# Four gated layers on one core: the first stage's loads and normalising move to ScalarE, and the last attention clears ahead, keeps GpSimd in written order and splits keys from queries

## The chip, the core and the metric

The kernel runs on one core of a Trainium2 chip. The core has five engines, each of which runs its own stream of instructions in order: TensorE (PE in the profile, with its weight loads as PEld), VectorE (DVE), ScalarE (ACT), GpSimd (POOL) and SyncE (SP, which here only issues DMAs). They wait for each other through semaphores. Plain loads and stores are issued by SP and ScalarE; gathers by index are issued by GpSimd. The metric is the device time of one execution, in microseconds.

## The reference, cut to what matters

Sixteen sequences of 128 tokens with 256 features (`x`) pass four layers. Each layer adds a cross part and then a feed-forward part to `x`, each scaled by the tanh of a gate:

```python
x = x + tanh(g_xattn[0]) * L0_xattn(ctx, ctx, layernorm(x), ssm_kernel, D, 8)   # first stage
x = x + tanh(g_ffn[0])   * L0_ffn(layernorm(x), ...)                            # experts
x = x + tanh(g_xattn[1]) * L1_xattn(layernorm(x), ctx, ctx, mask, ...)
x = x + tanh(g_ffn[1])   * L1_ffn(layernorm(x), ...)
x = x + tanh(g_xattn[2]) * L2_xattn(layernorm(x), ctx, ctx, decay)
x = x + tanh(g_ffn[2])   * L2_ffn(layernorm(x), ...)                            # experts
x = x + tanh(g_xattn[3]) * L3_xattn(layernorm(x), ctx, ...)                     # channel attention
x = x + tanh(g_ffn[3])   * L3_ffn(layernorm(x), ...)
```

Two of them matter here. The first stage forms, for each head of 8 features, all 64 products of context features, runs a causal convolution over the 128 tokens with the head's kernel (plus `D` times the input), and contracts the result with the normalised `x` as query. The channel attention takes the transposed view: each of the 16 heads has 8 of the 128 token rows as channels, and attends from 256 feature positions to 256 feature positions:

```python
q, k, v = Wq @ x + bq, Wk @ c + bk, Wv @ c + bv      # per sequence, [128, 256]; x normalised
scores = einsum('bhkt,bhks->bhts', q, k) / sqrt(8)   # 16 heads, 8 channels, 256 x 256
out = Wo @ (softmax(scores) applied to v) + bo
```

The queries come from `x`, the keys and values from the context alone.

## The kernel before, in words

**The frame.** The program holds `x` in SBUF as four groups `xg[g]` of four sequences each. The body, `passage`, is written twice: a first time with softmax sums watched for range, and a second time, under a condition on the result, with a search for the maxima (`search`). On these inputs only the first runs; "search" branches are not executed. Outside blocks marked `manual_schedule`, a planner orders each engine's instructions by its own estimate of their costs. Inside such a block, the engines named there keep the order in which the code is written, and the planner orders the others. Tiles come from pools with a number of buffers; an instruction that writes a buffer waits until the last reader of its former content is done.

**First stage (`stage_l0x`, L200 to L312; the planner orders it).** SP issues the four loads of `x` (L93), constants (L99), and four loads of the padded kernels (L213) into `rev`, which shares memory with `oT`. ScalarE issues the two loads of the transposed context (L95), 1 MB each, and then applies Tanh to the gates (L113). TensorE reverses the kernels by a product with a flipped identity (L225, two heads each), ScalarE copies the result into `toep` (L226), VectorE adds `D` to its diagonal (L237). `layernorm` (L149) takes mean and variance of one group on VectorE (L155, L156), the reciprocal root on GpSimd (L160), and normalises on VectorE (L163) into `xn`; TensorE transposes `xn` (L234) and ScalarE copies it into `qT` (L235). Then the loop over 16 heads: GpSimd multiplies the context features (`kv`, L289), TensorE convolves (L297, twelve products of 512 columns a head) into `y` with three buffers in PSUM, VectorE multiplies by `qT` of all sequences (`pr`, L302) and reduces (L305). In between come the mask rows (L246 to L262) and key rows (L267, L269) for a later layer. At the end the result is transposed back and added to `x` (L310, L312).

**Channel attention (`stage_l3x`, L1478 to L1784; TensorE, VectorE and ScalarE keep the written order, the planner orders GpSimd and SP).** Its input still lacks the experts' output of the stage before, which lies in DRAM and is gathered here (`fetch`, L709, two gathers a sequence; three buffers of `yc`). For sequence `b`: `stats` adds the gathered rows (L1524) and takes statistics (L1527 to L1530); `rsqrt` is the reciprocal root on GpSimd (L1535); `normal` normalises (L1541); `project` makes queries and keys (L1553, L1554) into one PSUM tile; `biased` adds the biases (L1559, L1560); `halves` splits both into a rounded part (ScalarE, L1566) and its remainder (GpSimd, L1567) and writes them by four DMAs to the DRAM buffer `scr` (L1571, L1573); `spread` reads them back by four DMAs into `qas` and `kas` (L1589), in the layout that a head's product needs. These, and `vbuf` for the values, have three buffers; each must be zero outside the written rows, so `clear` (L1546 to L1549) zeroes each once and sets a column of ones in `vbuf`, from whose product the softmax sums come. `project_v` and `keep_v` make the values.

Each sequence has eight steps `u`. In each, `weigh` makes scores (L1660) into one of two PSUM buffers and ScalarE takes their exponential into `pt` (L1667). `values` multiplies by the values (L1676) once for every two steps; `keep_values` copies the result to `avs` (L1687); `back` transposes (L1692), `normalise` divides by the sums, `turn`, `output` and `store` bring the result to `x` (L1707 to L1725). Two tables say what else is issued at step `u` of sequence `b`: `taken` ahead of the step's scores, `made` behind them; `(halves, 3)` stands for `halves(b + 3)`:

```python
for n in range(-40, 8 * B + 17):
    b, u = divmod(n, 8)
    for f, d, *r in taken[u]: when(f, b + d, *r)
    if 0 <= n < 8 * B: weigh(n)
    for f, d, *r in made[u]: when(f, b + d, *r)
```

So the loop starts five sequences ahead, and TensorE's first scores stand behind the projections of the first three sequences.

Of the kernel before, what the change touches and what calls it, by code (L numbers as in the profile page):

```python
# [55 lines left out]
def passage(ctx: ExitStack, tc: tile.TileContext, a: dict, out: bass.AP, inv, flag):  # L56
# [56 lines left out]
    nc.scalar.activation(tg, tg, AF.Tanh)  # L113

# [34 lines left out]
    def layernorm(pool, g, extra=None, tag="xn"):  # L149
# [10 lines left out]
        nc.gpsimd.tensor_tensor(rs, ve, neghalf, ALU.pow)  # L160
        xn = pool.tile([P, GB, D], F32, name="xn", tag=tag)
        for k in range(GB):
            nc.vector.tensor_scalar(xn[:, k, :], x[:, k, :], mv[:, k, 0:1], rs[:, k : k + 1], ALU.subtract, ALU.mult)  # L163
# [36 lines left out]
    def stage_l0x(ka, vbuf, anyk):  # L200

        with tc.tile_pool(name="s0", bufs=1) as s0, tc.tile_pool(name="s0w", bufs=2) as s0w, tc.tile_pool(
# [9 lines left out]
            for q in range(4):  # L212
                nc.sync.dma_start(  # L213
                    rev[:, 4 * q : 4 * q + 4, :],
                    bass.AP(tensor=kp.tensor, offset=kp.offset + 4 * q * W, ap=[[1, P], [W, 4], [1, D]]),
                )
# [6 lines left out]
            for h in range(0, B, 2):  # L223
                t = pst.tile([P, 2 * D], F32, name="tp")
                nc.tensor.matmul(t, lhsT=flip, rhs=rev[:, h : h + 2, :].rearrange("p h s -> p (h s)"), start=True, stop=True)  # L225
                nc.scalar.copy(T[:, h : h + 2, :].rearrange("p h s -> p (h s)"), t)  # L226
            dsk = s0.tile([P, B], F32, name="dsk")
# [1250 lines left out]
    def stage_l3x(wn, bn, wv, won, bov, pos, wgt, ys):  # L1478
# [8 lines left out]
        with tc.tile_pool(name="l3", bufs=1) as l3, tc.tile_pool(name="l3w", bufs=2) as w_, tc.tile_pool(  # L1487
# [4 lines left out]
            engines={mybir.EngineType.PE, mybir.EngineType.DVE, mybir.EngineType.Activation}  # L1492
# [3 lines left out]
            scr = [l3d.tile([8, P, D], F32, name=f"scr{i}") for i in range(NB)]  # L1496
# [7 lines left out]
            def begin(b):  # L1504
                fetch(b)
# [37 lines left out]
            def clear(b):  # L1543

                if b < NB:
                    nc.vector.memset(qas[b].bitcast(F32), 0.0)  # L1546
                    for t in (kas[b].rearrange("p j t -> p (j t)"), vbuf[b].rearrange("p s h k -> p (s h k)")):
                        nc.scalar.activation(t, ones[:, 0:1].to_broadcast(list(t.shape)), AF.Copy, scale=0.0)
                    nc.gpsimd.memset(vbuf[b][:, :, :, 8:9], 1.0)  # L1549

            def project(b):
                ps["f", b] = t = psa.tile([P, 2, D], F32, name="qk", tag="a")
                nc.tensor.matmul(t[:, 0, :], lhsT=wn[0], rhs=xns.pop(b), start=True, stop=True)  # L1553
                nc.tensor.matmul(t[:, 1, :], lhsT=wn[1], rhs=cbs[b], start=True, stop=True)  # L1554

            def biased(b):
                t = ps.pop(("f", b))
                fs[b] = f = w_.tile([P, 2, D], F32, name="f")
                nc.vector.tensor_scalar(f[:, 0, :], t[:, 0, :], bn[0], SC, ALU.add, ALU.mult)  # L1559
                nc.vector.tensor_scalar(f[:, 1, :], t[:, 1, :], bn[1], None, ALU.add)  # L1560

            def halves(b):

                f = fs.pop(b)
                hl = w_.tile([P, 2, 2, D], F32R, name="hl")
                nc.scalar.copy(hl[:, :, 0, :], f)  # L1566
                nc.gpsimd.tensor_tensor(hl[:, :, 1, :], f, hl[:, :, 0, :].bitcast(F32), ALU.subtract)  # L1567
                s = scr[b % NB]
                hf = hl.bitcast(F32)
                for x in range(2):  # L1570
                    nc.sync.dma_start(s[2 * x : 2 * x + 2].rearrange("s p t -> p s t"), bc(hf[:, 0, x], 1, 2))  # L1571
                for x in range(2):
                    nc.sync.dma_start(s[4 + 2 * x : 6 + 2 * x].rearrange("s p t -> p s t"), hf[:, 1])  # L1573

            def spread(b):

                s = scr[b % NB]
                for h in range(2):
                    r = slice(64 * h + 32, 64 * h + 34)
                    if not search:  # L1580
                        continue
                    if b < NB:
                        nc.sync.dma_start(kas[b][r].bitcast(F32), bc(ones[0:2, :], 1, 16))
                    else:
                        nc.sync.dma_start(qas[b % NB][r].bitcast(F32), bc(zr, 1, 16))
                s = s.rearrange("s (k h) t -> (s k) (h t)", h=16)
# [478 lines left out]
```

## Time and profile before

| | us |
|---|---|
| median of 3 runs (lowest, highest) | 1079.42 (1078.66, 1079.55) |
| the profiled execution | 1077.04 |
| its span, first to last instruction | 1075.3 |
| first stage (0 to 138): PE, DVE, ACT, POOL busy | 111.6, 111.0, 17.0, 77.5 |
| channel attention (752 to 972): PE, DVE, ACT, POOL busy | 182.8, 107.2, 155.4, 72.2 |
| its entry (752 to 787): PE, DVE, ACT, POOL busy | 8.0, 14.1, 10.4, 16.4 |
| its steady part (800 to 905): PE, DVE, ACT, POOL busy | 99.6, 58.5, 81.2, 39.9 |
| mean granted TensorE clock | 0.904 |

A row of the timeline has the start in us, the duration in us, the engine, the line of the kernel, the operation, what it writes and reads, the shapes, a count of merged instructions, and in brackets how long the engine idled before it and what ended that. The windows give busy time per engine in a stretch. The chain is the work that ended last, followed back from the end. A matmul's end is modelled; GpSimd's times are rough.

### The profile page before, as it was taken

To read this page: it belongs to the slowest core of one execution; us is meant where nothing else is said; L and a number is where in the kernel's file an instruction comes from. 1 tells how busy PE (TensorE), PEld (TensorE's weight loads), DVE (VectorE), ACT (ScalarE), POOL (GpSimd) and SP (SyncE) were. 2 spreads that over 40 slices of the span, in tenths; PEclk is the share of its full clock that TensorE was granted. 3 is DMA by queue.
4 is the path that set the end of the run, shared out by engine and by line. 5 is a ranking of instruction groups with operands and counts; after the bars stand their busy time and mean duration, and the time that the engine had idled before them with its cause. 6 is when DMAs were issued, how large, how long until landed. Compare 5 with 4: busy or idle time off the path is not lost. (4 is left out here: it accounts for less than half of the span.)

```text
span 1075.3 us, 14892 instructions
## 1 busy us (share of the span) xinstructions
PE 904.1 (84%) x5212; PEld 602.5 (56%) x5212; DVE 607.5 (56%) x1537; ACT 456.8 (42%) x707; POOL 342.3 (32%) x389
## 2 busy tenths in 40 slices
PE   3899978899999888888864858998169999998797
PEld 1444456677778444455443747887145555555564
DVE  5988966322225656787788586454345555534442
ACT  1211024223322446666762242454257777882111
POOL 5766322543115324211111046550443342201000
PEclk9999979999999978999986557899579999997999
DMA  9100070233341109800000202352488887530000
GB/s 305 41 1 1 0 220 21 63 104 109 69 143 50 39 20 144 78 1 1 1 1 1 78 1 88 109 145 82 142 247 235 220 222 195 164 79 1 20 30 32
DMA packets 71401, 94.12 MB, mean 88 GB/s; under 512 B 9271, under 2 KB 63127, under 8 KB 69015
## 3 DMA queue, kind: packets, MB, share of 16 engines
q1 hardware_dynamic: 56952, 67.21, 21.1%
q0 software_dynamic: 14080, 23.78, 11.4%
q10 hardware_dynamic: 288, 2.10, 0.5%
q8 instruction: 45, 0.74, 0.3%
q14 instruction: 36, 0.29, 0.1%
HBM read 57.06 MB, written 33.55 MB: 84 GB/s over the span
## 5 line engine op out<-in xcount | busy, mean ns | idle before, releaser
L1667 ACT ACTIVATE pt<-s 128x1024 f32<-128x1024 f32 x128 | 126.4, 1024 | 32.5 <-PE s L1660 29.8
L709 POOL DMA_INDIRECT yc<-ys,pos x64 | 62.4, 975 | 125.0 <-DVE x L729 49.2
L297 PE MATMUL y<-kv,toep 128*128 128x512 f32 x192 | 86.6, 602 | 1.6 <-DVE toep L237 1.6
L1660 PE MATMUL s<-qa,ka 64*128 64x256 f32 x512 | 64.3, 332 | 8.3 <-ACT pt L1667 7.5
L1676 PE MATMUL av<-pt,v 128*32 128x256 f32 x1024 | 69.4, 389 | 0.1
L289 POOL TENSOR_TENSOR kv<-ctxT 128x1024 f32<-128x1024 f32 x32 | 60.2, 1900 | 28.3 <-PE y L297 28.3
L1660 PEld LDWEIGHTS s<-qa,ka 64*128 64x128 f32 x512 | 38.6, 188 | 46.9 <-issue 23.2
L1687 DVE COPY avs<-av 128x256 f32<-128x256 f32 x64 | 27.1, 423 | 65.5 <-PE av L1676 48.5
L297 PEld LDWEIGHTS y<-kv,toep 128*128 128x128 f32 x192 | 35.6, 192 | 43.7 <-issue 40.3
L616 PE MATMUL ub<-L0we,xbT 128*128 x160 | 50.8, 460 | 2.6 <-ACT xbT L607 2.6
L593 POOL DMA_INDIRECT xb<-xs,who x40 | 38.2, 954 | 43.3 <-PE tb L605 33.2
L913 PE MATMUL yb<-L2we,hT 88*128 (+1 forms) x224 | 41.7, 315 | 9.6 <-DVE hT L737 3.9
L848 POOL DMA_INDIRECT xb<-xs,who x40 | 38.1, 953 | 31.7 <-PE tb L860 20.9
L302 DVE TENSOR_TENSOR pr<-y,qT 128x1024 f32<-128x1024 f32 x32 | 39.0, 1222 | 12.1 <-PE y L297 9.4
L1567 POOL TENSOR_TENSOR hl<-f,hl 128x512 fp32r<-128x512 f32 x16 | 20.5, 1282 | 79.5 <-ACT hl L1566 79.5
L477 PE MATMUL up<-L0s,xT 128*128 128x352 f32 x128 | 43.0, 482 | 0.0
L913 PEld LDWEIGHTS yb<-L2we,hT 88*128 88x128 f32 x224 | 33.6, 205 | 16.5 <-DVE hT L737 9.0
L1086 PE MATMUL s<-qa,ka 18*128 18x512 f32 x128 | 37.4, 660 | 4.9 <-ACT follow L1380 4.9
L305 DVE TENSOR_REDUCE oT<-pr 128x128 f32<-128x1024 f32 x32 | 38.9, 1219 | 1.0
L1676 PEld LDWEIGHTS av<-pt,v 128*32 128x32 f32 x1024 | 26.9, 110 | 20.4 <-issue 0.7
L642 PE MATMUL yb<-L0we,hTb 88*128 x160 | 37.9, 379 | 0.0
L616 PEld LDWEIGHTS ub<-L0we,xbT 128*128 128x128 f32 x160 | 28.8, 190 | 15.5 <-ACT xbT L607 2.8
(384 smaller groups left out, 2043.1 us busy)
## 6 DMA issues: line engine op xcount, KB each, us to landing
scr<-hl SPq DMA_DIRECT2D x64, 256.0 KB
ys<-ysb SPq DMA_DIRECT2D x40, 256.0 KB
qa<-scr SPq DMA_DIRECT2D x32, 256.0 KB
ka<-scr SPq DMA_DIRECT2D x32, 256.0 KB
L2we<-in_L_w_dram POOLq DMA_DIRECT2D x6, 792.0 KB
L0we<-in_L_w_dram SPq DMA_DIRECT2D x6, 704.0 KB
xs<-xn SPq DMA_DIRECT2D x8, 512.0 KB
x<-in_x_dram SPq DMA_DIRECT2D x4, 512.0 KB
```

The source lines that it names most:

```text
L289: nc.gpsimd.tensor_tensor(t, bc(ch, 3, 8), bc(ch, 2, 8), ALU.mult)
L297: nc.tensor.matmul(y[:, ns], lhsT=T[:, h, d : d + P], rhs=kv[mc][:, ns], start=(mc == 0), stop=(mc == lc))
L302: nc.vector.tensor_tensor(pr, y.rearrange("p (b j i) -> p b j i", b=B, j=8), bc(qT[:, lc, :, hs], 2, 8), ALU.mult)
L305: nc.vector.tensor_reduce(oT[:, lc, :, hs], pr, AX.X, ALU.add)
L477: nc.tensor.matmul(t[:, n, 0 : 2 * I], lhsT=xT[:, c, b * P : (b + 1) * P], rhs=s13[:, c, n, :], start=(c == 0), stop=(c == 1),)
L593: nc.gpsimd.indirect_dma_start(out=xbs[s][:, i, :], out_offset=None, in_=xs, in_offset=bass.IndirectOffsetOnAxis(ap=who[:, 2 * s + i : 2 * ...
L616: nc.tensor.matmul(t[:, i, 0 : 2 * I], lhsT=xbT[:, i, c, :], rhs=we[:, bass.ds(regs[s][i] + c * 2 * I, 2 * I)], start=(c == 0), stop=(c == 1),
L709: nc.gpsimd.indirect_dma_start(out=got[b][:, i, :], out_offset=None, in_=ys, in_offset=bass.IndirectOffsetOnAxis(ap=pos[:, i, b : b + 1], ...
L913: nc.tensor.matmul(y[:, i, :], lhsT=hT[:, x, k, i, :], rhs=we[0:HI, bass.ds(at[i] + 4 * I + k * D, D)], start=(n == 0), stop=(n == 3),)
L1660: nc.tensor.matmul(s[:, h, jj, :], lhsT=ka[r, 2 * i + jj, sc * P : (sc + 1) * P], rhs=qa[r, 2 * i + jj, :], start=True, stop=True,)
L1667: nc.scalar.activation(pts[b, i][:, sc], s, AF.Exp)
L1676: nc.tensor.matmul(av[c : c + 32, :], lhsT=va[:, sc, 8 * h + 2 * i + jj, :], rhs=pt[:, sc, h, jj, :], start=(sc == 0), stop=(sc == 1),)
```

## The change

- **First stage.** The four kernel loads are issued by ScalarE instead of SP. `layernorm` computes `nb = -mean * root` on VectorE (one small instruction a group) and normalises on ScalarE, as Identity with scale `rs` and bias `nb`. The Tanh of the gates is written behind the copies of the reversed kernels.
- **Channel attention, order.** GpSimd joins the engines that keep the written order. The three `clear` calls stand in front of the loop, and their ones column is set by a step of its own, `marked`, at step 6. `begin` is split: the context load comes one sequence earlier (`context`, 5), the gather stands behind the root of the sequence before it (`rsqrt`, 3, then `fetch`, 4).
- **Channel attention, keys apart.** `project`, `biased`, `halves` and `spread` take a second argument, 1 for keys and 0 for queries, with a PSUM tile, an `f`, an `hl` (four buffers) and two writes to `scr` each. Keys are projected at step 0 and queries at step 2; keys run one sequence ahead of queries. `scr` has four buffers. For the first three sequences the keys are spread at step 3 (`ahead`), later ones together with the queries (`behind`), two sequences ahead as before.

```diff
-    nc.scalar.activation(tg, tg, AF.Tanh)
-
...
+        nb = small.tile([P, GB], F32, name="nb")
+        nc.vector.scalar_tensor_tensor(nb, mv[:, :, 0], -1.0, rs, ALU.mult, ALU.mult)
         xn = pool.tile([P, GB, D], F32, name="xn", tag=tag)
         for k in range(GB):
-            nc.vector.tensor_scalar(xn[:, k, :], x[:, k, :], mv[:, k, 0:1], rs[:, k : k + 1], ALU.subtract, ALU.mult)
+            nc.scalar.activation(
+                xn[:, k, :], x[:, k, :], AF.Identity, bias=nb[:, k : k + 1], scale=rs[:, k : k + 1]
+            )
...
             for q in range(4):
-                nc.sync.dma_start(
+                nc.scalar.dma_start(
                     rev[:, 4 * q : 4 * q + 4, :],
...
                 nc.scalar.copy(T[:, h : h + 2, :].rearrange("p h s -> p (h s)"), t)
+            nc.scalar.activation(tg, tg, AF.Tanh)
...
-            engines={mybir.EngineType.PE, mybir.EngineType.DVE, mybir.EngineType.Activation}
+            engines={
+                mybir.EngineType.PE,
+                mybir.EngineType.DVE,
+                mybir.EngineType.Activation,
+                mybir.EngineType.Pool,
+            }
...
-            scr = [l3d.tile([8, P, D], F32, name=f"scr{i}") for i in range(NB)]
+            NS3 = NB + 1
+            scr = [l3d.tile([8, P, D], F32, name=f"scr{i}") for i in range(NS3)]
...
             def begin(b):
-                fetch(b)
+                if search:
+                    fetch(b)
+                context(b)
+
+            def context(b):
                 cbs[b] = w_.tile([P, D], F32, name="cb", bufs=3 if search else 4)
                 nc.sync.dma_start(cbs[b], a["ctx"][b])
...
+                    if search:
+                        marked(b)
+
+            def marked(b):
+                if b < NB:
                     nc.gpsimd.memset(vbuf[b][:, :, :, 8:9], 1.0)
 
-            def project(b):
-                ps["f", b] = t = psa.tile([P, 2, D], F32, name="qk", tag="a")
-                nc.tensor.matmul(t[:, 0, :], lhsT=wn[0], rhs=xns.pop(b), start=True, stop=True)
-                nc.tensor.matmul(t[:, 1, :], lhsT=wn[1], rhs=cbs[b], start=True, stop=True)
...
+            def project(b, x):
+                ps["f", b, x] = t = psa.tile([P, D], F32, name="qk", tag="a")
+                nc.tensor.matmul(t, lhsT=wn[x], rhs=cbs[b] if x else xns.pop(b), start=True, stop=True)
...
+            def halves(b, x):
+
+                f = fs.pop((b, x))
+                hl = w_.tile([P, 2, D], F32R, name="hl", bufs=4)
+                nc.scalar.copy(hl[:, 0, :], f)
+                nc.gpsimd.tensor_tensor(hl[:, 1, :], f, hl[:, 0, :].bitcast(F32), ALU.subtract)
+                s = scr[b % NS3]
                 hf = hl.bitcast(F32)
-                for x in range(2):
-                    nc.sync.dma_start(s[2 * x : 2 * x + 2].rearrange("s p t -> p s t"), bc(hf[:, 0, x], 1, 2))
-                for x in range(2):
-                    nc.sync.dma_start(s[4 + 2 * x : 6 + 2 * x].rearrange("s p t -> p s t"), hf[:, 1])
...
+                for i in range(2):
+                    at = 4 * x + 2 * i
+                    nc.sync.dma_start(
+                        s[at : at + 2].rearrange("s p t -> p s t"), hf if x else bc(hf[:, i], 1, 2)
+                    )
...
+            def ahead(b):
+
+                if b < NB:
+                    spread(b, 1)
+
+            def behind(b):
+                if b >= NB:
+                    spread(b, 1)
+                spread(b, 0)
...
                 taken = (
-                    ((begin, 4), (rsqrt, 3), (keep_values, -1, 2), (spread, 2)),
-                    ((normal, 3), (clear, 3)),
-                    ((keep_values, -1, 3),),
-                    ((normalise, -1, 0), (normalise, -1, 1), (biased, 3)),
-                    ((keep_values, 0, 0), (halves, 3)),
+                    ((context, 5), (rsqrt, 3), (fetch, 4), (keep_values, -1, 2), (behind, 2)),
+                    ((normal, 3), (biased, 4, 1)),
+                    ((keep_values, -1, 3), (halves, 4, 1)),
+                    ((normalise, -1, 0), (normalise, -1, 1), (biased, 3, 0), (ahead, 4)),
+                    ((keep_values, 0, 0), (halves, 3, 0)),
                     ((keep_turned, -1, 0), (keep_turned, -1, 1)),
                     ((keep_values, 0, 1), (keep_v, 2)),
                     ((store, -1), (stats, 4)),
                 )
                 made = (
-                    (),
+                    ((project, 4, 1),),
                     ((values, -1, 3),),
-                    ((back, -1, 0), (back, -1, 1), (project, 3)),
+                    ((back, -1, 0), (back, -1, 1), (project, 3, 0)),
                     ((values, 0, 0),),
                     ((turn, -1, 0), (turn, -1, 1)),
                     ((values, 0, 1), (project_v, 2)),
-                    ((output, -1),),
+                    ((output, -1), (marked, 3)),
                     ((values, 0, 2),),
                 )
+                for b in range(NB):
+                    clear(b)
```

## The prediction

> **What bounds the kernel now.** I first read the slices of the page, each 26.9 us long.
>
> ```profile
> PE   3899978899999888888864858998169999998797
> ```
>
> TensorE is the fullest engine nearly everywhere. The holes that the change can reach are the first slice and slice 28 (753 to 780 us), the entry of the channel attention. So I read the timeline and the waits of three stretches. The start:
>
> ```profile
> 18.22 10.52 DVE L163 TENSOR_SCALAR xn<-x,mv,rs 128x256 f32<-128x256 f32 x8
> ...
> 18.66 9.35 PE L225 MATMUL tp<-oT,flip 128*128 128x512 f32 x16 [18.66 <-DMA oT<-in_kpad_dram]
> ...
> 41.52 12.18 PE L297 MATMUL y<-kv,toep 128*128 128x512 f32 x28
> ...
> 41.90 1.22 DVE L302 TENSOR_TENSOR pr<-y,qT 128x1024 f32<-128x1024 f32 x1 [2.12 <-ACT qT L235]
> ```
>
> TensorE waits for the reversed kernels until 18.66. Eight normalisings take VectorE 10.52 us, 1.3 each, while GpSimd multiplies (kv, four of 1.9 from 19.03 on); without it they take 0.40. The last queries are ready at 41.87, and only then does VectorE begin to drain y. The windows say what binds from there:
>
> ```profile
> 42.00:60.00 18.00, 18.00 (x45) 7.75 (x43) 17.12 (x17) 0.36 (x1) 13.31 (x10) 1.00 0.00 1
> 60.00:80.00 20.00, 20.00 (x47) 8.45 (x48) 16.66 (x15) 3.23 (x8) 12.78 (x7) 1.00 0.00 0
> ```
>
> (Columns: window, length, busy PE, PEld, DVE, ACT, POOL, clock, DMA share, GB/s.) TensorE is full until 126.9 us, so what brings 41.9 forward brings the stage's end forward. Next the chain that ended last, at the channel attention:
>
> ```profile
> 756.03 0.95 POOL yc L709
> ...
> 764.80 0.95 POOL yc L709
> 765.77 0.60 POOL rs L1535
> ...
> 774.36 0.60 POOL rs L1535
> ```
>
> The first reciprocal root starts at 765.77 although its input was ready at 761.77 (L1530): GpSimd was issuing gathers for later batches. Then one batch (one sequence b) takes 8.6 us (765.77, 774.36, 782.92, 791.54). TensorE's first score stands behind batch 2's projection and starts at 786.87. Last, one steady batch (timeline around 895 us):
>
> ```profile
> 894.31 1.07 PE L1676 MATMUL av<-pt,v 128*32 128x256 f32 x16
> ...
> 896.73 0.42 DVE L1687 COPY avs<-av 128x256 f32<-128x256 f32 x1 [2.21 <-PE s L1660]
> ...
> 896.85 2.86 ACT L1667 ACTIVATE pt<-s 128x1024 f32<-128x1024 f32 x3 [1.03 <-PE s L1660]
> ...
> 897.92 0.50 PE L1660 MATMUL s<-qa,ka 64*128 64x256 f32 x4 [0.55 <-ACT pt L1667]
> ```
>
> The value products end at 895.38, but VectorE takes them at 896.73, and ScalarE takes the scores of 895.32 at 896.85. TensorE's word seems held back beside the second gather (POOL L709 at 895.23, 0.95 long), and TensorE then loses 0.55 us. Batches with this gather repeat every 11.73 us (u=2 at 816.20, 827.93, ... 898.36); without one, from batch 10, every 11.12 (907.05, 918.17), with nothing lost.
>
> **The skill.** "ScalarE: Activation LUTs", What ACT_TABLE_LOAD costs: 186 ns plus 0.833 ns a column, 93 for each pointer operand, 93 of overlap. That gives an estimate of 0.585 us for the new normalising; the nearest row, L1723 (bias and scale from tiles), has 0.56 and follows-on at 0.45. They agree. "SBUF — State Buffer", SBUF: two separate sides: GpSimd and some VectorE operations take a shared port pair exclusively; the 1.3 against 0.40 us agree. "DMA: Bandwidth & Descriptors", Issuing engines are not separate DMA queues: a second issuer saves issue time only; the DMA share of 1.0 to 1.1 from 8 to 28 us agrees. Its section Queues, rings and completion order says that an engine goes round its queues packet by packet; I use that for the kernels' bytes, and no row of the page shows two 1 KB streams at once.
>
> **First stage.** Four kernel loads (1.17 to 1.41 us of issue, from 10.15) leave SP for ScalarE, idle behind its two ctxT issues (1.7 us). Should a full queue hold an issue there, as it held the fourth of x on SP for 5.79 us, ScalarE still has nothing else to do until about 15. SP's later loads move 5.2 us forward. At 350 GB/s (windows 12:20), x, ctxT and kernels (6.3 MB) can't be in before about 21 us either way, so kernels come sooner and x later. Estimate: ctxT is through at about 11 us; kernels and x then share. First kernels land near 14.8 instead of 18.6, last near 23.8; x of group 3 lands near 22.5. Its statistics (four of 0.40) end at 24.3, the root (1.03, perhaps behind one 1.9 product) at 25.4 to 27.3, nb (0.2). ScalarE now carries, at follow-on spacing, 8 toep copies of 0.49, 16 normalisings of 0.47, 8 qT copies of 0.49 and Tanh with its table (1.5): 16.8 us from about 16.6, so the last qT copy ends at 33.4 at the earliest. Tanh was free at 10.96 and now costs its 1.5 if it precedes that copy. VectorE loses 16 normalisings, gains 4 small nb, each of which waits for GpSimd's root with the next group's statistics and the 16 diagonal additions (0.27, L237) queued behind it; those and the two row operations (1.33, 1.31) fit before 34, and at worst they cost their 7 us. I take 34: **minus 8 us**. Bounds: minus 12 (ScalarE never bound, chain of x alone, 30) and 0 (the planner of this stage orders ScalarE badly).
>
> **Entry of the attention.** The clears of three batches go in front: VectorE 3 x 1.77 = 5.3 us from 752, hidden before the first gathered rows (759.90; without that cover, 5.3 us); ScalarE 3 x (1.91 + 1.04) from 752.5, ends 761.1 with overlap. The first key copy stands behind that (0.4), GpSimd's key remainder behind it (0.7, from 1.28 for twice the size), and in the fixed order the first root behind that: 762.4 instead of 765.77. The ones column is 3 memsets of 0.17, moved in GpSimd's queue; free. Now a gather of batch b+1 is issued after the root of b, so its latency enters the recurrence: root 0.60, gap 0.16, then 5.74 from gather issue to ve (756.03 to 761.77), 0.1: 6.6 us against 8.6. The other branch (root, xn 0.41, one projection 1.22, bias 0.48, copy 0.4, remainder 0.7, gaps) is 4.3 and hidden. Roots at 762.4, 769.0, 775.6; xn of batch 2 0.8 later, its projection 1.22, project_v 1.06: first score at 778.8 against 786.87. The projection of batch 3 ends at 784.5 against 794.6. DMA is 0.94 to 1.00 busy at 775 to 785 and will be pressed harder, so of 8 to 10 I take **minus 8 us**; bounds minus 10 and minus 3.
>
> **Steady batches.** Eight writes and reads through scr and q, k per batch stay, from SP; the key half leaves earlier, with a fourth scr and two more hl buffers. ScalarE's split costs 0.41 x 2 - 0.61 = 0.2, GpSimd's 0.73 x 2 - 1.28 = 0.2 per batch; they are 77% and 38% busy from 800 to 905, so free. TensorE's pieces by start to start: 8 scores of 0.43, 4 value products of 1.00, back 0.92, projections 0.43 and 0.53, turn 0.36, tv 0.65, output 0.63: 11.0. The key projection moves between scores 0 and 1, so score 2 comes 0.5 later and back plus query no longer starve ScalarE (1.09 us each batch). The gather moves from just before score 0 to behind the root: store's addition (0.73) after ys (-0.4 from score 0), root to +1.1, gathers at +1.3 and +2.5. The value products that back needs end at +2.4, just ahead. If their word passes, the copy (0.42) precedes back, what is held is score 2, which has 1 us of slack, and batches 1 to 9 go from 11.73 to about 11.2: **minus 4 us** after rounding down. Held until 1.5 us after the second gather's start, as now, it stalls back by 1.65: 12.75 a batch, 12 batches, plus 11 to 12 us.
>
> Sum: -8 - 8 - 4 = -20. The profiled execution took 1077.04 us (span 1075.3, 1.7 around it); it goes to 1057.0. The median of the runs is 2.4 above it, so **1059.4**. What follows either stage is chained to its end, and nothing there changes.
>
> **Rivals.** (1) The hold lands on the last values: -16 + 12 gives 1075; for it, the margin is 0.1 us; against it, gathers at 205 and 361 us hold nothing visible. 20%. (2) ScalarE becomes the first stage's bound and gives all back: -12, 1067; for it, 16.8 us of work in a 17 us space; against, VectorE's 10.52 us are truly gone. 15%. (3) Slower: the same hold, longer. At 207 us three words of TensorE come out together about 2.4 us late (ScalarE's L485 idles 4.24 until 210.14). With 2.6 us of stall a batch takes 13.7: +23 - 16, 1086. It decides from 13.07 us a batch on, where 12 batches eat 16 us. 12%. (4) It doesn't do what it says, the planner leaving the stage's order and GpSimd's order as they were: 1079, 3%. (5) The steady batches at 11.1 and both other gains at their bounds: 1052, 5%. The forecast itself: 45%.
>
> Faster: forecast, 1, 2, 5: 0.85. Same (within 0.2%, 2.2 us, about what a measurement here can tell from no change): 0.03. Slower: 0.12. The range 1050 to 1078 leaves out rival 3 and the far ends; the forecast's own is 1053 to 1066.
>
> **What would show it.** Right: first y drained (L302) at 32 to 36; TensorE full from there; first score 778 to 782; root to root 6.5 to 7.2 us at the entry; scores' period 11.1 to 11.3, no 0.55 before score 2. Wrong: qT late behind xn or Tanh on ScalarE; the copy of the fourth value product idling 1.4 us beside a gather, with back waiting for it; the first roots still 8.6 apart.

## The result, and the profile after

The changed kernel takes 1072.05 us (median of 20 runs, 1066.92 to 1079.37) against 1079.35 (20 runs, 1075.77 to 1083.19): a ratio of 0.9935 [0.992, 0.995], so 7.3 us less where 20 were forecast. The profiled execution after has a span of 1073.2 us (before 1075.3).

The slices of its page:

```profile
PE   3999978899999987888865858799469999998797
```

Counted from 0, slice 28 went from 1 to 4, in part because the channel attention starts 5.5 us later in this execution, and slice 29 is 6 as before: the hole at its entry is smaller, not closed. The timeline of the first stage after (L215 is the issue of the kernels' loads, L227 the reversal, L228 its copy, L156 the variance, L158 the root, L160 `nb`, L238 the copy into `qT`, L251 the mask rows, L261 a small diagonal, L305 the first drain of `y`, that is VectorE's first product from it):

```profile
1.74 14.87 ACTq L215 DMA_DIRECT2D oT<-in_kpad_dram  x4
...
16.64 1.28 ACT L228 ACT_TABLE_LOAD   x1 [16.64 <-DMA x<-in_x_dram]
...
20.54 5.39 PE L227 MATMUL tp<-oT,flip 128*128 128x512 f32 x8 [2.88 <-DMA oT<-in_kpad_dram]
...
22.46 0.59 ACT L228 COPY toep<-tp 128x512 f32<-128x512 f32 x1 [2.27 <-PE tp L227]
...
22.92 1.07 DVE L156 TENSOR_SCALAR ve<-mv 128x4 f32<-128x4 f32 x1
...
27.66 1.80 POOL L282 MEMSET v<- 128x2048 f32 x1
...
32.04 1.04 POOL L158 TENSOR_TENSOR rs<-ve,neghalf 128x4 f32<-128x4 f32 x1
...
33.11 0.24 DVE L160 SCALAR_TENSOR_TENSOR nb<-mv,rs 128x4 f32<-128x4 f32 x1 [3.14 <-POOL rs L158]
...
33.64 1.99 POOL L292 TENSOR_TENSOR kv<-ctxT 128x1024 f32<-128x1024 f32 x1
...
33.80 2.91 DVE L251 TENSOR_SCALAR rows<-rows,consts 2x2048 f32<-2x2048 f32 x1
...
37.95 1.07 ACT L238 COPY qT<-tp 128x512 f32<-128x512 f32 x2 [0.62 <-PE tp L237]
...
39.12 1.83 DVE L261 TENSOR_SCALAR diag<-ident,some 16x16 f32<-16x16 f32 x1
...
40.87 1.20 DVE L305 TENSOR_TENSOR pr<-y,qT 128x1024 f32<-128x1024 f32 x1
```

The last group's statistics are ready at 24.0, but its root starts at 32.04: GpSimd had the clearing of `vbuf`, mask loads and constants ahead of it. The queries end at 39.0 instead of 42.4, and VectorE, whose row operation took 2.91 us beside GpSimd's product, still has a small diagonal ahead of the drain, which starts at 40.87, one us before the old 41.90. The windows behind it:

```profile
42.00:60.00 18.00, 18.00 (x37) 7.66 (x36) 15.06 (x16) 0.30 (x1) 9.85 (x6) 0.83 0.00 1
60.00:80.00 20.00, 20.00 (x48) 8.36 (x47) 18.36 (x16) 2.93 (x8) 12.66 (x7) 1.00 0.00 0
```

TensorE is full, but from 42 to 60 us with a granted clock of 0.83 (0.62 from 42 to 50), which takes 3 us in this execution. GpSimd at the attention's entry, and the reason of its third root:

```profile
767.39 0.58 POOL L1548 TENSOR_TENSOR rs<-ve,neghalf 128x1 f32<-128x1 f32 x1
...
773.76 0.57 POOL L1548 TENSOR_TENSOR rs<-ve,neghalf 128x1 f32<-128x1 f32 x1 [1.83 <-DVE ve L1543]
...
780.57 0.48 DVE L1537 SCALAR_TENSOR_TENSOR x<-yc,wgt,x 128x256 f32<-128x256 f32 x1 [3.86 <-DMA yc<-ys,pos]
...
782.94 0.56 POOL L1548 TENSOR_TENSOR rs<-ve,neghalf 128x1 f32<-128x1 f32 x1 [4.64 <-DVE ve L1543]
...
786.07 0.79 PE L1687 MATMUL s<-qa,ka 64*128 64x256 f32 x4
```

Roots are 6.4, 9.2 and 8.0 us apart (the fourth is at 790.94); the third waits for gathered rows. The first score comes 24.6 us after the first gather (761.51), before it was 30.8. A steady batch after:

```profile
848.12 1.07 PE L1703 MATMUL av<-pt,v 128*32 128x256 f32 x16
849.03 0.96 POOL L712 DMA_INDIRECT yc<-ys,pos  x1 [0.31 <-issue]
...
849.55 0.55 PE L1719 MATMUL ta<-ident,avs 128*128 128x128 f32 x3
...
849.78 0.42 DVE L1714 COPY avs<-av 128x256 f32<-128x256 f32 x1 [1.33 <-PE s L1687]
...
850.26 0.77 PE L1719 MATMUL ta<-ident,avs 128*128 128x128 f32 x5 [0.15 <-issue]
...
850.59 1.03 ACT L1694 ACTIVATE pt<-s 128x1024 f32<-128x1024 f32 x1 [1.04 <-PE ta L1719]
```

The last values end at 849.19, 0.16 us after the second gather has started, and VectorE takes them only at 849.78; ScalarE idles 1.04. Below, "held" means this delay of about 0.6 us where it is 0.07 us at the batch's other values. TensorE itself goes on meanwhile (849.55), so it is its word that comes late or is late to be taken; the trace doesn't tell which. A batch with gathers takes 11.58 us (before 11.73).

Between 140 and 750 us the three engines' work is in the same order in both traces, yet this stretch took 6.6 us longer in this one execution. So it had to be found out whether that belongs to the change.

### The profile page after: what moved, and what is told of

Read it like the earlier page. It is cut to its first block, busy times and chain, and to the rows that moved or that the text cites. A ratio compares the mean times of both kernels' runs of the same rounds, so it can differ in the third digit from the quotient of the medians.

```text
span 1073.2 us, 14994 instructions
## 1 busy us (share of the span) xinstructions
PE 912.4 (85%) x5212; PEld 602.3 (56%) x5212; DVE 605.2 (56%) x1525; ACT 467.8 (44%) x739; POOL 343.3 (32%) x405
## 5 line engine op out<-in xcount | busy, mean ns | idle before, releaser
L916 PE MATMUL yb<-L2we,hT 88*128 (+1 forms) x224 | 42.2, 317 | 11.5 <-ACT hT L739 5.3
L305 DVE TENSOR_TENSOR pr<-y,qT 128x1024 f32<-128x1024 f32 x32 | 38.9, 1219 | 10.6 <-PE y L300 10.2
L1047 PE MATMUL tq<-xT,l1q 128*128 128x256 f32 x128 | 35.0, 421 | 2.4 <-ACT xT L1038 2.4
```

The costliest lines, as they stand in the source:

```text
L305: nc.vector.tensor_tensor(pr, y.rearrange("p (b j i) -> p b j i", b=B, j=8), bc(qT[:, lc, :, hs], 2, 8), ALU.mult)
L916: nc.tensor.matmul(y[:, i, :], lhsT=hT[:, x, k, i, :], rhs=we[0:HI, bass.ds(at[i] + 4 * I + k * D, D)], start=(n == 0), stop=(n == 3),)
```

## The experiments

Each ratio is to the kernel before on the same chip; the runs are spread over several chips, on which before took 1063.6 to 1080.1 us. "Stage end" is the end of the last addition to `x` in the first stage.

**Each part alone.** `first_alone` has the first stage's edits on the kernel before, `attn_alone` the attention's.

> The first stage's part alone (kernels' loads and normalising on ScalarE, Tanh later); the attention is as before. Additive theory (each part is worth what its own stage shows, and the 6.6 us that the middle lost in the one profiled execution are variation between executions): first pr at about 40.9 us instead of 41.9, last x of the stage at 136.6 instead of 137.7, so 1.1 us less in all: about 1078.2 beside 1079.35, ratio 0.999. Rival (the first stage's part costs the stages behind it 5 to 6 us, by another order or clock): 1083 to 1085, ratio 1.004 to 1.006, with the middle (137 to 752 us) longer than before by as much in this execution too.

> The attention's part alone; the first stage is as before. Additive theory: entry (first gather to first score) 24.6 us instead of 30.8, last score 205 us after the first gather instead of 212.6, so 7.5 us less: about 1071.9, ratio 0.993, and with the first stage's 1.1 the whole change's 0.9935 is explained. Rival (the attention's part is worth 12 or more, and the first stage's part takes 5 back): 1067, ratio 0.989.

`first_alone`: 0.9985 [0.9969, 1.0001]; `attn_alone`: 0.9939 [0.9916, 0.9963]. Their product is 0.9924, within the interval of the whole change: they add up, and no loss in the middle is needed to explain it. Stage end 133.64 against 137.69, 4.05 us sooner although the first drain is only 1.03 sooner: before that drain TensorE now finishes all three buffers of `y` (16 records of products by 42 us against 10; an estimate from them is 6 x 0.43 = 2.6 us). Of the 4.05 us, 2.7 are left when the experts' gathers start (193.27 against 195.95). One stretch on the way, from 160 to 170 us, first `attn_alone`, then `first_alone`:

```profile
160.00:170.00 10.00, 10.00 (x58) 8.49 (x57) 4.60 (x15) 4.33 (x8) 1.90 (x3) 0.83 0.19 64
```

```profile
160.00:170.00 10.00, 10.00 (x39) 8.02 (x39) 5.19 (x15) 2.26 (x5) 0.73 (x1) 0.66 0.00 0
```

TensorE is full in both, at a granted clock of 0.83 and 0.66: 1.7 us, about what is missing. That is one execution each; I don't know what decides when the clock is lowered. The attention: last score 200.35 us after the first gather against 207.07, 6.7 less, of it 6.3 at the entry. Batches take 11.19 against 11.12: on this chip before loses nothing beside its gathers.

**The changed kernel again.**

> The changed kernel itself, once more. Theory that what the middle lost (6.6 us between 137 and 752 us) and the 3 us at 42 to 50 us (granted clock 0.62) belong to that one execution: first pr at 40.8 to 40.9, last convolution at 123.6 as in the kernel with the first stage's part alone, the middle (stage end to first gather of the channel attention) 611 to 613 us, ratio 0.992 to 0.994. Theory that the hold beside the second gather belongs to the chip or to the execution and not to the code: batches of 11.2 us with gathers. Rival, that all three belong to the changed kernel: last convolution at 126.8, the middle at 625, batches of 11.6.

> The changed kernel itself for the comparison: ratio to before 0.992 to 0.996; batches of 11.58 us if the chip holds TensorE's signals (then before has 11.73), 11.19 if not; the middle (stage end to the attention's first gather) between 611 and 625 us by the granted clock.

0.9965 [0.9931, 1.0] and 0.9934 [0.9913, 0.9955], on two chips. The clock of 42 to 50 us was 0.64 and 1.00, stage end 136.41 and 132.80. From there to the attention's first gather, where no kernel differs from another, the twenty profiles of all runs take 608.9 to 617.7 us on the two chips where before takes 1064 us, and 618.3 to 624.9 on the others (before 618.3, first after 624.9, `after_third` 620.8). So both losses of the first profile vary between executions. Batches: 11.19 in the first, 11.55 in the second. With the others: in 12 profiled executions on chips where before takes 1077 to 1080 us, TensorE's signals are held beside the second gather; in 8 on two chips where it takes 1064, never. In `attn_alone`, one of these eight, whose attention is that of the change, the values that end at 832.19 beside a gather started at 832.02 are taken at 832.25. What it is in the chips, no run shows. `first_alone` has the attention of before, and its copy beside the gather is released in time (before, VectorE idled 2.21 there):

```profile
833.95 0.94 POOL L712 DMA_INDIRECT yc<-ys,pos  x1 [0.30 <-DMA scr<-hl]
...
834.17 0.43 DVE L1690 COPY avs<-av 128x256 f32<-128x256 f32 x1 [0.94 <-PE av L1679]
```

**First stage: the late root.**

```diff
-    nc.gpsimd.memset(vbuf, 0.0)
+    behind_of(nc.gpsimd.memset(vbuf, 0.0), roots[-1])
```

The mask loads, the constants and the third product are put behind that root in the same way.

> The changed kernel, with one order added in the first stage: GpSimd's fourth root stands behind its third product, ahead of the clearing of vbuf, the mask loads and the sorter's constants. Theory that this root, late by some 6 us (ve at 24.0, root at 32.0), is what kept the last queries until 39.0: root at about 26, last qT copy at 35.5 to 36.5 (ScalarE then is the limit), first pr at 36.5 to 37.5 instead of 40.9, the stage's end 3.5 to 4.5 us sooner: about 1068, ratio to before 0.989 to 0.990. Rival, that ScalarE is the limit by itself: last qT copy stays at 38.5 to 39 and the time at 1072. Rival, that VectorE's row and diagonal operations (L251, L254, L261: 5.95 us in the changed kernel) hold the first pr: qT ready by 36.5, but first pr at 39 or later, 1070 to 1071.

0.9904 [0.9882, 0.9926]. Root, queries and drain (timelines of GpSimd, ScalarE and VectorE):

```profile
26.16 1.12 POOL L168 TENSOR_TENSOR rs<-ve,neghalf 128x4 f32<-128x4 f32 x1 [0.41 <-DVE toep L250]
```

```profile
37.88 1.07 ACT L248 COPY qT<-tp 128x512 f32<-128x512 f32 x2 [0.62 <-PE tp L247]
```

```profile
38.50 2.36 DVE L319 TENSOR_TENSOR pr<-y,qT 128x1024 f32<-128x1024 f32 x2 [1.18 <-ACT qT L248]
```

The root is 6 us earlier, the last `qT` copy is not (38.95): ScalarE's order was full. But VectorE is done with its rows early, and drains at 38.50: stage end 131.31, 2.33 sooner than `first_alone`.

One execution of each is not enough for that size. `lead`, `clears_loop`, `sp_order`, `entry` and `split` below leave the changed first stage as it is; over the nine profiles that have it, the stage ends between 131.60 and 136.61 (median 133.06) and the first drain lies between 39.03 and 40.93. The two kernels with the early root and nothing else new in this stage, `root_early` and `root_split`, end it at 131.31 and 131.26, so the root is worth about 1.8 us. Half clock from about 41 to 48 us is one reason for the spread (136.41 and 136.61 have it). Another is a race near 33.7 us. In six of the nine GpSimd's product starts 0.1 to 0.2 us before VectorE's row operation, which then takes 2.9 us. In `sp_order`, `entry` and `split` VectorE is first: its operation takes 1.33 us, the product 4.6 to 5.0 us, and the drain comes at 39.03 to 39.59, late root or not.

**Rows out of the way**: `root_early`, with the row operations and the small diagonal behind the first reduction.

```diff
+    behind_of(nc.vector.tensor_scalar(rows, rows, rsc, rbi, ALU.mult, ALU.add), drained[0])
```

> As root_early, and besides VectorE's row operations and the small diagonal stand behind the first reduction of pr, away from the queries' path. If the root alone is the cause: as root_early within 0.5 us (first pr 36 to 37). If VectorE's row operations hold the first pr: first pr 2 to 4 us ahead of root_early's, and the stage's end with it.

0.9927 [0.9909, 0.9945]: drain at 39.79, where `qT` ended 1.3 later than in `root_early`; stage end 133.36. No gain: with the root early, the rows were already hidden.

**The loads.** `loads_sp` puts the kernels' loads back on SP; `ctx_behind` is `root_early` with `ctxT` issued by SP behind `x`.

> The changed kernel with the four kernels' loads back on SP behind x; normalising stays on ScalarE. Theory that in the first stage the order written by the planner (fourth root behind GpSimd's constants, copies of the reversed kernels behind the normalising) and not the loads decides: last qT copy at 38.5 to 39.5, first pr within 0.7 us of 40.8, ratio 0.992 to 0.996 as the changed kernel. Rival, that the earlier kernels are what the first stage gained from: first pr at 42 or later, the stage's end 2 to 4 us later than 133 to 136, ratio 0.996 to 1.0.

> As root_early (fourth root early), and besides the two ctxT loads issued by SP behind x instead of by ScalarE ahead of the kernels' loads. Theory that ScalarE, with 16.8 us of work behind the last kernels, is the first stage's limit after the root, and that these loads decide when it starts: kernels and x landed by about 14 us, reversing and normalising 5 to 8 us sooner, last qT copy at 31 to 33 instead of 39.0, GpSimd's first products at 20 to 21; first pr at 32 to 34, the stage's end 5 to 7 us ahead of root_early's 131.3; ratio 0.984 to 0.987. Rival, that ctxT and the products of GpSimd (four of 1.9 us, then y) become the limit: first pr at 36 or later, ratio 0.989 to 0.990 as root_early.

`loads_sp`: 0.9921 [0.9896, 0.9946], drain at 40.08, stage end 132.93 (`after_third` 132.80): the move of the loads is worth nothing here. The issue times and semaphores of the first trace after show how little it moved. Only the first kernel load is issued at once (1.74). The second, third and fourth each wait for a semaphore that a load of `x` raises: `x` landed at 12.40, 14.71 and 16.21, and they were issued at 12.42, 14.73 and 16.24. So the kernels land at 14.00, 20.41, 22.20 and 25.27, where before they land at 18.52, 20.03, 21.54 and 23.03 (in `loads_sp` 18.53 to 23.04): one quarter sooner, three later.

`ctx_behind`: 0.9916 [0.9902, 0.993], drain at 39.22. Here all four loads are issued by 3.42 us:

```profile
0.81 2.61 ACTq L225 DMA_DIRECT2D oT<-in_kpad_dram  x4
```

The first kernels land at 6.7, 7 us sooner, the last at 17.8, and nothing comes of it (ScalarE, then TensorE):

```profile
18.73 0.60 ACT L173 ACTIVATE xn<-x,nb,rs 128x256 f32<-128x256 f32 x1 [11.21 <-DVE nb L170]
...
19.33 0.58 ACT L173 ACTIVATE xn<-x,nb,rs 128x256 f32<-128x256 f32 x1
19.82 0.56 ACT L238 COPY toep<-tp 128x512 f32<-128x512 f32 x1
```

```profile
20.44 2.08 PE L237 MATMUL tp<-oT,flip 128*128 128x512 f32 x2 [9.83 <-ACT toep L238]
```

The planner had put two normalisings ahead of the first copy, and `nb` behind all statistics on VectorE; the reversals wait 9.83 us for a PSUM buffer.

**Written order, and less on ScalarE.** `ordered` is `ctx_behind` with reversals first and the groups in turn (the lines are shortened; it also puts the third and fourth root ahead of GpSimd's products, `y` behind the third group's transposes, the mask rows behind the first reduction and the key rows two heads later); `halved` is `root_early` with two of four normalisings back on VectorE.

```diff
+            with tc.manual_schedule(engines={PE, DVE, Activation}):
+                for h in range(0, B, 2): reverse(h)
+                nc.scalar.activation(tg, tg, AF.Tanh)
+                for g in range(NG):
+                    if g + 1 < NG: mv[g + 1] = layer_stats(g + 1)
+                    for h in range(4 * g, 4 * g + 4): diagonal(h)
+                    queries(g, *mv[g])
```

> ctx_behind, with TensorE, VectorE and ScalarE in written order up to the queries (reversals first, then group by group statistics, nb, normalising, transposes, copies), the third and fourth root ahead of GpSimd's products, and the row operations behind the first reduction. Theory that the planner's order, not the work on ScalarE, kept the last qT copy at 39: the last qT copy at 26 to 29, first pr at 27 to 30 instead of 40.9, the stage's end 9 to 13 us ahead of the changed kernel's 133 to 136.5; ratio 0.981 to 0.985 (a part may be lost again behind the stage, as 1.5 of 4.1 us were). Rival, that ScalarE's 16.8 us or GpSimd's products bind: first pr at 34 or later, ratio 0.988 or more.

> As root_early, with two of each group's four normalisings back on VectorE and two on ScalarE. If ScalarE's work is the first stage's limit: 8 x 0.5 = 4 us less on ScalarE, last qT copy at 35 to 36.5 instead of 38.95, first pr at 36 to 37.5 instead of 38.5, the stage's end 1 to 2.5 us ahead of root_early's 131.3; ratio to before 0.988 to 0.990. If VectorE's work beside GpSimd's products (1.3 us a normalising as before) is what was saved by the change: first pr at 39.5 or later, ratio 0.992 or more.

`ordered`: 0.9928 [0.9911, 0.9944]; `qT` ends at 37.94:

```profile
20.27 0.58 ACT L246 COPY toep<-tp 128x512 f32<-128x512 f32 x1 [0.27 <-PE tp L245]
...
20.86 2.06 ACT L178 ACTIVATE xn<-x,nb,rs 128x256 f32<-128x256 f32 x4
...
31.53 3.62 PE L340 MATMUL y<-kv,toep 128*128 128x512 f32 x4
...
36.87 1.07 ACT L261 COPY qT<-tp 128x512 f32<-128x512 f32 x2 [2.54 <-PE tp L260]
```

Now the copies wait for kernels that land up to 18.3, and the normalisings stand behind them; then TensorE, at half clock from 25.6 to 35.8 us (0.9 us a record), puts `y` ahead of the last transposes. `halved`: 0.9936 [0.9912, 0.9961], `qT` at 39.03: ScalarE is busy 14.05 of the 22.5 us before 39.1 (17.84 in `root_early`), but VectorE is slow again beside GpSimd's products:

```profile
20.69 3.97 DVE L174 TENSOR_SCALAR xn<-x,mv,rs 128x256 f32<-128x256 f32 x2
```

2.0 each, and 0.36 where GpSimd rests (33.23, 0.72 for two). So no single engine's load was shown to be the limit; in all variants run the queries end between 36.9 and 40.5.

**The entry.** `lead` gathers one sequence further ahead, `clears_loop` puts the clears back into the loop, `sp_order` has SP in written order, `entry` combines the first and the last with contexts in front and the first key reads later.

```diff
-    (rsqrt, 3), (fetch, 4)
+    (rsqrt, 3), (fetch, 5)
...
+                mybir.EngineType.SP,
```

The first edit is that of `lead`, the second that of `sp_order`.

> The changed kernel with the gathers one sequence further ahead (fetch, 5 instead of fetch, 4, still behind the root), so that a gather's latency no longer lies between two roots of the entry. Theory that this latency sets the entry: roots 3 to 4.5 us apart instead of 6.4, 9.2 and 8.0, the first score 6 to 10 us sooner than 24.6 us after the first gather, ratio 0.985 to 0.988. Rival, that the DMA engines set it (busy 0.94 to 0.99 from 752 to 800 us with the writes and reads of scr): the first score at most 2 us sooner, 0.991 to 0.994.

> The changed kernel with the three clears put back into the loop, one behind each of the first three key copies (step 2) instead of all in front. Theory that the clears in front hold the first key copy and with it the first root (ScalarE clears until 4.8 us after the first gather, the first root comes 5.9 us after it): first root 2 us sooner and the first score 1.5 to 2.5 us sooner, ratio about 0.991. Rival, that the gathers' landings set the first score, not the first root: first score within 0.5 us of 24.6 us after the first gather, or later, since the clears now stand between the sequences' copies.

> The changed kernel with SP too in written order in the channel attention, so that the first queries' read (spread, 0) no longer stands behind the next sequences' writes. Theory that this queue sets the entry (the first qa read was issued 9 us after its remainder was ready, and the first score waited 3.55 us for it): the first score 4 to 7 us sooner, 18 to 20.5 us after the first gather instead of 24.6, ratio 0.987 to 0.990. Rival, that the roots or the DMA engines' load set it: first score at 23.5 to 25 us after the first gather, ratio as the changed kernel.

> The changed kernel with gathers one sequence further ahead, SP in written order, the first four context loads in front and the first key reads behind the next query writes. If SP's order holds the first score once the roots come earlier: first query read issued 13 to 15 us after the first gather instead of 20, first score at 18 to 21 us after the first gather instead of 24.6; ratio 0.986 to 0.990. If the DMA engines' load holds it: writes to scr take 5 us to land as before, first score at 23 us or later, ratio as the changed kernel's (0.992 to 0.997).

| | ratio | roots, us after the first gather | first score | last score |
|---|---|---|---|---|
| changed, `after_again` | 0.9965 | 6.0, 12.4, 21.8 | 24.9 | 202.5 |
| `lead` | 0.9922 [0.9904, 0.9941] | 5.9, 11.8, 17.7 | 24.4 | 200.9 |
| `clears_loop` | 0.9968 [0.9949, 0.9987] | 7.6, 15.8, 22.2 | 26.0 | 203.3 |
| changed, `after_third` (held) | 0.9934 | 5.9, 12.4, 21.4 | 24.5 | 205.0 |
| `entry` (held) | 0.9925 [0.9902, 0.9947] | 5.9, 11.8, 17.7 | 21.0 | 205.4 |
| `sp_order` (held) | 0.9963 [0.9952, 0.9974] | 5.9, 13.2, 21.4 | 25.0 | 210.4 |

`lead` brings the third root 4 us forward and the first score not at all. Its score waits for queries whose read SP issued 20 us after the first gather:

```profile
760.41 3.55 SPq L1592 DMA_DIRECT2D scr<-hl  x4
...
766.85 0.79 SPq L1606 DMA_DIRECT2D qa<-scr  x2
...
771.15 0.55 PE L1687 MATMUL s<-qa,ka 64*128 64x256 f32 x1 [3.55 <-DMA qa<-scr]
```

`entry` issues that read at 16.3 and its first score is 3.5 us sooner, but the first sequence's result is turned back 41.5 us after the first gather, as in `after_third`. What was won is lost at once: in TensorE's order a key projection stands behind the first scores, and its context, issued by SP at 776.51, lands late.

```profile
780.74 1.19 PE L1575 MATMUL qk<-cb,l3kn 128*128 128x256 f32 x2 [5.39 <-DMA cb<-in_ctx_dram]
```

The DMA engines' mean share is 1.04 from 765 to 780 us there, so their load is the likely limit, with SP's order as the rival; no run took bytes away. `sp_order` alone makes the context loads late (TensorE waits 5.91, 4.91 and 6.56 us for them). The clears in front cost nothing: with them back in the loop the first score comes 1.1 us later than in `after_again`.

**The hold.** `split` is `lead` with the second gather four steps behind the first.

```diff
-    ((context, 5), (rsqrt, 3), (fetch, 4), (keep_values, -1, 2), (behind, 2)),
+    ((context, 5), (rsqrt, 3), (fetch, 5, 0), (keep_values, -1, 2), (behind, 2)),
...
-    ((keep_values, 0, 0), (halves, 3, 0)),
+    ((keep_values, 0, 0), (halves, 3, 0), (fetch, 5, 1)),
```

> The changed kernel with gathers one sequence further ahead and the second of the two gathers moved four steps behind the first. On a chip that holds TensorE's signals beside the second gather (batches of 11.58 us with the changed kernel): if it takes two gathers in a row, 11.2 us a batch and 4 us less in all; if a single gather holds as well, 11.58 or more. On a chip without the hold: 11.19 us a batch in either case, and the ratio of the kernel lead (0.992).

0.9921 [0.9894, 0.9949] on a chip with the hold; batches of 11.19, last score at 200.7. The second gather still holds the signal, where nothing is urgent:

```profile
843.01 1.07 PE L1705 MATMUL av<-pt,v 128*32 128x256 f32 x16
843.16 0.97 POOL L714 DMA_INDIRECT yc<-ys,pos  x1
...
844.50 0.42 DVE L1716 COPY avs<-av 128x256 f32<-128x256 f32 x1 [1.43 <-PE av L1705]
```

The values end at 844.08 and are taken at 844.50; at the first gather (848.26) nothing is late. So a gather need not follow another to hold a signal; whether it costs anything depends on which signal is due beside it. The lead alone doesn't help: `entry` and `best`, on chips with the hold, have 11.5 to 11.6 us in most of their batches.

**Combinations.** `best` is `ordered`, `lead` and `sp_order`; `best2` is `halved` and `entry`; `root_split` is `root_early` and `split`.

> ordered, with the attention's gathers one sequence further ahead (as in lead) and SP in written order (as in sp_order). If the entry is set by the queue of SP and then by the latency of the gathers between two roots: first score 15 to 18 us after the first gather; both stages together 0.972 to 0.979. If the DMA engines set the entry, first score 21 us or more after the first gather: 0.980 to 0.985.

> halved and entry together. If both are what they are expected to be and add up: 0.980 to 0.985; if only the first stage's part is worth its gain: 0.987 to 0.991; if neither: 0.990 to 0.995.

> The changed kernel with the early fourth root (root_early) and with the gathers one sequence further ahead and four steps apart (split). If they add up: 2.3 us at the first stage's end, and in the attention 4 us on a chip with the hold (batches of 11.19 instead of 11.58) or 0 to 1.6 us on one without it; ratio to before 0.986 to 0.990, and 3 to 6 us less than the changed kernel on the same chip. If the gain at the first stage is given back behind it: within 2 us of the changed kernel on a chip without the hold.

0.9974 [0.9957, 0.9991], 0.9933 [0.9909, 0.9957] and 0.9886 [0.9862, 0.9909]. `root_split` took 1064.01 us where the changed kernel took 1069.34 and before 1077.13: 5.3 us less than the change, with stage end at 131.26 and 11.19 a batch. Its ratio is the lowest of all kernels run, though the interval of `root_early` overlaps; `best` and `best2` fall short of what was expected of them.

## Why the prediction was wrong

The direction held, the size did not: 7.3 us for 20, and each of the three terms was too large.

**First stage, minus 8: 4 at its end, 1.6 (-0.1 to 3.3) in the time.** The step that failed is "the last qT copy ends at 33.4 at the earliest", taken as 34: it ended at 39.0, and at 38.95 with the early root. The forecast summed ScalarE's own 16.8 us. In the trace ScalarE has 17.86 us of work between 16.6 and 39.1, and 4.5 us of waits that the sum put at nothing. Of these, 2.27 are for a reversal whose kernels landed only at 20.41; most of the rest is for reversals and transposes on TensorE, which alternate with ScalarE through two PSUM buffers. This is the weak form of rival 2, without giving all back. Which wait ends last once the kernels are early, no variant settled.

Two steps ahead of it failed too. That "kernels come sooner and x later" held for the first quarter of the kernels alone (14.8 forecast, 14.00 landed): the other loads waited for `x`, whose last group came at 18.26 and not 22.5. A full queue was considered there, a semaphore was not; what held the fourth load of `x` on SP, the traces don't say. That the statistics were ready when forecast (24.3; 24.0) is luck: VectorE lost 2.5 us at the third `nb`, 0.66 waiting for its root and 1.84 beside GpSimd's product. And "the root (1.03, perhaps behind one 1.9 product) at 25.4 to 27.3" started at 32.04, behind all that the planner put there. In before the mask loads and constants stood behind that root; I took that order as given. Its delay costs about 1.8 us at the stage's end, as far as the traces show through VectorE's rows and not through the queries. "What brings 41.9 forward brings the stage's end forward" was wrong in the other direction: the end came 4.05 us sooner for a drain 1.03 sooner, since three buffers of `y` were full by then.

**Entry, minus 8: minus 6.3.** The first root (6.4 us after the gather; 5.9) and the second's distance (6.6; 6.4) were right. The recurrence then failed: the gathers' 5.74 us were taken as fixed, but the third pair of rows landed late (9.2 and 8.0), perhaps for the keys' and contexts' traffic, which no run took away. The third root, at 21.4 us after the first gather for 19.6, makes up the 1.8 us that are missing in the forecast's terms. But `lead` shows that a second chain (write to `scr`, SP's queue, read) was as long; the prediction had only the first, and looked at the DMA engines for a discount alone.

**Steady batches, minus 4: minus 1.2 with the hold, minus 0.4 without.** These are first to last score: 181.8 to 180.5, and 176.3 to 175.8; a batch went from 11.73 to 11.58, and from 11.12 to 11.19. The sum of TensorE's pieces, 11.0, was right: 11.19 is what TensorE alone needs, and `split` reaches it on a chip with the hold. The failed step is "if their word passes": the second gather starts at +2.40 and the values end at +2.56, so the margin of 0.1 us was lost, and their word is held. Rival 1 happened, but at 0.4 us a batch (11.58 - 11.19): the copy is taken 0.75 us after the gather's start and not 1.5, and back then stalls 0.15, not 1.65. On a chip without the hold there was nothing to win.

## What to carry to other kernels

Before forecasting what a moved operation frees, write out the order of every in-order engine that the chain passes, the planner's too: a ready root waited 8 us behind constants. Look up what the issue of a moved load waits for: three of four loads on a free engine stood behind the loads that they were to overtake. Give a size only when several profiles of one kernel agree on it: nine of the same first stage ended 5 us apart. Price engines that alternate by their waits for each other, not by the work of one. A loss that stands beside a DMA issue in one profile may belong to that chip; put where no signal was urgent, the issue cost nothing on a chip that has the loss.

## What was not expected of the hardware

TensorE's signals are taken late, up to 1.35 us after the modelled end (before, 895.38 to 896.73), beside the second gather of each pair on some chips (12 executions) and not on others (8). VectorE's normalising of 128x256 takes 0.36 to 2.0 us, by what GpSimd does. The Trainium skill, "SBUF — State Buffer", SBUF: two separate sides, says that GpSimd and some VectorE operations share a pair of ports, which the one that starts first keeps for its whole instruction; the 2.0 us agree, and so do the row operation's 1.33 us where it starts first and 2.9 us where GpSimd's product does. The granted TensorE clock was 0.62 and 0.64 over 8 us of full work in two executions of the changed kernel and 1.00 in a third, which is a difference of 3 us.
